# A gated cross-attention block: the keys' bias scaled behind the first statistics, transposes of the identity ahead of the tokens' ones, and block 1's tokens loaded sooner

## The chip, the cores and the metric

The kernel runs on one core of a Trainium2 chip. A core has five engines with queues of their own: TensorE (PE in the profile, with its weight loads as PEld), VectorE (DVE), ScalarE (ACT), GpSimd (POOL) and SyncE (SP), which here only issues DMA transfers. ScalarE issues a few transfers too. An engine takes its instructions in order; between engines there are semaphores. The metric is device microseconds of one execution, lower is better.

## The reference, cut to what matters

Tokens x are two sequences of 2048 rows with 512 features; the context has 77 rows per sequence. There are 16 heads of 32.

```python
x = x + tanh(g_xattn) * attention(layernorm(x), ctx, ctx)   # Wq, Wk, Wv, Wo with biases
x = x + tanh(g_ffn)   * ffn(layernorm(x))

# attention
q = layernorm(x) @ Wq.T + bq;  k = ctx @ Wk.T + bk;  v = ctx @ Wv.T + bv
out = softmax(q k.T / sqrt(32)) v @ Wo.T + bo

# ffn: both linear layers on integers, one scale for a whole tensor
def qlinear(x, w, b):
    sx, sw = max|x| / 127, max|w| / 127
    return (round(x / sx) @ round(w / sw).T + b) * (sw * sx)
out = qlinear(gelu(qlinear(x, w1, b1)), w2, b2)
```

Since the scale of a tensor is its greatest magnitude over all tokens, the whole attention has to be done before the first product of the feed-forward part, and that before the second product.

## The kernel before, in words

The 4096 tokens are eight blocks of 512 (`TB`), a block being four tiles of 128 rows. The first four blocks are the first sequence. Attention is computed in float32. For each block there are eight steps, two for each group of four heads: scores (`scores`, row ps in the profile), the least of them (mx), the exponential (e) on ScalarE, the sums and their reciprocals (sm, rs) on VectorE, the shares on GpSimd (row L561), their transposes through TensorE (pta), the product with the values (pc), and the product with Wo (oa, ob). Two steps are in flight. The feed-forward part follows: first product (ph), GELU, and then the second (pf).

In the attention part the order of every engine, SP's queue with it, is the order in which the code is written (a manual schedule). An instruction whose operand is late holds all that stands behind it on its engine. That holds for GpSimd above all here: its queue is strictly in order of the text.

The start, as the code has it:

- Loads. SP and ScalarE issue block 0's tokens in four pieces (`load_x(0, pieces=NT, ...)`), ScalarE then the context of sequence 0, `bk_sb` and `bq_sb` (2 KB each). SP goes on with column groups of Wk and Wq (`load_group`), Wv, `bv_sb`, the last two groups of Wq, the context of sequence 1, block 1's tokens (`load_x(1)`), Wo, and small vectors. A transfer takes one of eight semaphores in turn, and the issue of one waits until the transfer eight places ahead has landed.
- Constants. GpSimd writes the identity (`make_identity`), which the transposes need, and clears the buffers of the keys.
- `nbk`, the keys' bias times minus the scale of the scores, is computed on GpSimd from `bk_sb` (line 755). Its only reader is `place_k` for the second sequence on ScalarE (line 253).
- A loop over the four tiles of block 0 (from line 757): `norm_stats(0, t)` takes mean and variance on VectorE (st_a, mv) and the inverse sigma on GpSimd (lines 174 and 175: ve_a, then rstd); `normalize(0, t - 1)` makes xn on VectorE; `transpose_x(0, t - 1)` transposes it in four pieces through TensorE (ptx, line 344) and ScalarE copies it out (line 345); at the third and fourth pass `project_k` makes a group of the keys (pk, line 236).
- Then the keys are placed (`place_k`, kb, line 255 on VectorE), the other groups made, and `project_q(0, 0)` makes the first queries (pq, line 353).

The banks of PSUM matter at two places. `pt` has two, used in turn by the token transposes and later by the shares' transposes. `project_k` and `project_q` take turns on two others (`bank`), so a new product waits until the one two places ahead has been read.

Weights for the feed-forward part are rounded beside the attention; their loads come behind those named.

Of the kernel before, what the change touches and what calls it, by code (L numbers as in the profile page):

```python
# [8 lines left out]
F32 = mybir.dt.float32  # L9
BF16 = mybir.dt.bfloat16  # L10
AF = mybir.ActivationFunctionType
ALU = mybir.AluOpType
# [3 lines left out]
P = 128  # L16
D = 512
KC = D // P
# [20 lines left out]
SCALE = float(DK) ** -0.5  # L39
# [3 lines left out]
def tile_flamingo_gated_block(  # L43
# [21 lines left out]
    nc = tc.nc  # L65
# [6 lines left out]
    small = ctx.enter_context(tc.tile_pool(name="small", bufs=4))  # L72

    def big(name):
        return xpool.tile([P, KC, TB], F32, tag="xblk", name=name)
# [3 lines left out]
    def load_x(i, pieces=1, engines=(nc.sync,)):  # L79
        X[i] = big(f"x{i}")  # L80
        src = x[i * TB : (i + 1) * TB, :].rearrange("(t p) d -> p t d", p=P)
        n = NT // pieces
        for t in range(0, NT, n):
            engine = engines[t // n % len(engines)]
            engine.dma_start(X[i][:, t : t + n, :], src[:, t : t + n, :])

    def kchunks(w):
        return w.rearrange("(kc p) n -> p kc n", p=P)
# [17 lines left out]
    bk_sb = const.tile([P, KC], F32, name="bk_sb")  # L106
# [6 lines left out]
    def load_group(engine, dst, src, g):  # L113
        c = slice(g * P, (g + 1) * P)
        engine.dma_start(dst[:, :, c], kchunks(src)[:, :, c])

    def load_ctx(engine, b):
        engine.dma_start(ctx_sb[b], kchunks(ctxT[b]))
# [10 lines left out]
    load_group(nc.sync, wq_sb, wqT, 1)  # L129
    nc.sync.dma_start(wv_sb, kchunks(wvT))  # L130
    nc.sync.dma_start(bv_sb, bv.to_broadcast([NK, D]))
    for g in range(2, NG):
        load_group(nc.sync, wq_sb, wqT, g)
    for b in range(1, B):
        load_ctx(nc.sync, b)
    load_x(1)
    xT_sb = {}

    def load_xT(i):
# [11 lines left out]
    ident = const.tile([P, P], F32, name="ident")  # L151
# [66 lines left out]
    with actx:  # L218
        ps_s = actx.enter_context(tc.tile_pool(name="ps_s", bufs=2, space=PSUM))
        ps_t = actx.enter_context(tc.tile_pool(name="ps_t", bufs=2, space=PSUM))  # L220
# [3 lines left out]
        def bank(name):  # L224

            turn[0] += 1
            return ps_p.tile([P, D], F32, tag=f"pp{turn[0] % 2}", name=name)
# [4 lines left out]
        def project_k(b, g):  # L232

            pk = bank(f"pk{b}_{g}")
            for kc in range(KC):
                nc.tensor.matmul(
                    pk[:, :NK],
                    wk_sb[:, kc, g * P : (g + 1) * P],
                    ctx_sb[b][:, kc, :],
                    start=(kc == 0),  # L240
                    stop=(kc == KC - 1),
                )
            return pk

        def place_k(b, g, pk):

            for j in range(HG):
                r = slice(j * DK, (j + 1) * DK)
                dst = kblk[b][r, g, j % RT * NK : (j % RT + 1) * NK]
                bias = bk_sb[r, g : g + 1]  # L250
                if j % 2 and b > 0:
                    bias = nbk[r, g : g + 1]
                    nc.scalar.activation(dst, pk[r, :NK], AF.Identity, bias=bias, scale=-SCALE)
                else:
                    nc.vector.tensor_scalar(dst, pk[r, :NK], bias, -SCALE, ALU.add, ALU.mult)
# [18 lines left out]
        def norm_stats(i, t):  # L274

            if t == 0:
                ln[i] = (
                    small.tile([P, NT, 2], F32, tag="mv", name=f"mv{i}"),
                    small.tile([P, NT], F32, tag="rstd", name=f"rstd{i}"),
                )  # L280
            mv, rstd = ln[i]
            tile_stats(mv[:, t, :], X[i][:, t, :], f"a{i}_{t}")
            if i == 0:
                inverse_sigma(rstd[:, t : t + 1], mv[:, t : t + 1, :], f"a{i}_{t}")
            elif t == NT - 1:
                inverse_sigma(rstd, mv, f"a{i}")
# [45 lines left out]
        def normalize(i, t):  # L332
            mv, rstd = ln[i]
            xn[i, t] = work.tile([P, D], F32, tag="xn", name=f"xn{i}_{t}")
            nc.vector.tensor_scalar(
                xn[i, t], X[i][:, t, :], mv[:, t, 0:1], rstd[:, t : t + 1], ALU.subtract, ALU.mult
            )

        def transpose_x(i, t):
            if t == 0:  # L340
                xnT[i] = work.tile([P, KC, TB], F32, tag="xnT", name=f"xnT{i}", bufs=2)
            pt = ps_t.tile([P, KC, P], F32, tag="pt", name=f"ptx{i}_{t}")
            for kc in range(KC):
                nc.tensor.transpose(pt[:, kc, :], xn[i, t][:, kc * P : (kc + 1) * P], ident)
            nc.scalar.copy(xnT[i][:, :, t * P : (t + 1) * P], pt)
# [405 lines left out]
                    else:  # L751
                        task[0](*task[1:])

        nbk = small.tile([P, KC], F32, tag="nbk", name="nbk", bufs=1)
        nc.gpsimd.tensor_scalar(nbk, bk_sb, -SCALE, None, ALU.mult)
        pk = {}
        for t in range(NT + 1):
            if t < NT:
                norm_stats(0, t)
            if t > 0:  # L760
                normalize(0, t - 1)
                transpose_x(0, t - 1)
            if t in (2, 3):
                pk[t - 2] = project_k(0, t - 2)
        place_k(0, 0, pk[0])
        pk[2] = project_k(0, 2)
        place_k(0, 1, pk[1])
# [193 lines left out]
    with ExitStack() as fctx:  # L961
# [23 lines left out]
        for i in range(NB):  # L985
# [4 lines left out]
            for a in range(GT):  # L990
                G = gtile(f"G{i}_{a}")
                for v in range(GF // 2):
# [25 lines left out]
                    n = 1 if k == NB * GT * 2 - 1 else 2  # L1018
# [24 lines left out]
    for i in ends:  # L1043
# [37 lines left out]
        for t in range(NT):  # L1081
# [3 lines left out]
            n = 2 if i == ends[-1] and t == NT - 1 else 1  # L1085
# [73 lines left out]
```

## Time and profile before

| | |
|---|---|
| times of three runs | 634.09, 634.13, 636.54 us (median 634.13) |
| the profiled execution | 637.02 us, its span 634.8 us |
| TensorE busy | 599.1 us, 94% of the span |
| VectorE, ScalarE, GpSimd busy | 75%, 65%, 52% |
| granted TensorE clock, mean | 0.986 |
| first matmul of TensorE starts | 9.85 us |
| first queries (pq) on TensorE | 18.58 to 22.64 us |
| attention ends, feed-forward begins | about 401 us |

How to read it: the span runs from the first to the last instruction; the execution's own time is 2.2 us longer. The chain that ended last names, piece by piece, the work or the wait that set the time. A row of the timeline gives the start and the length in microseconds, the engine, the line of the kernel, the operation, what is written and read with the shape, the number of instructions, and in brackets how long the engine had been idle and who released it. The granted clock is the share of TensorE's full clock that the hardware let through. Releasers are inferred, and a few matmul records can be missing.

### The profile page before, as it was taken

To read this page: it belongs to the slowest core of one execution; us is meant where nothing else is said; L and a number is where in the kernel's file an instruction comes from. 1 tells how busy PE (TensorE), PEld (TensorE's weight loads), DVE (VectorE), ACT (ScalarE), POOL (GpSimd) and SP (SyncE) were. 2 spreads that over 40 slices of the span, in tenths; PEclk is the share of its full clock that TensorE was granted. 3 is DMA by queue.
4 is the path that set the end of the run, shared out by engine and by line. 5 is a ranking of instruction groups with operands and counts; after the bars stand their busy time and mean duration, and the time that the engine had idled before them with its cause. 6 is when DMAs were issued, how large, how long until landed. Compare 5 with 4: busy or idle time off the path is not lost.

```text
span 634.8 us, 9361 instructions
## 1 busy us (share of the span) xinstructions
PE 599.1 (94%) x3269; PEld 372.1 (59%) x3290; DVE 477.6 (75%) x743; ACT 410.9 (65%) x922; POOL 330.6 (52%) x291
## 2 busy tenths in 40 slices
PE   3999999899999999999999969799999979999997
PEld 3556467677777777787787745344444424444444
DVE  4376658678998788777757686999999789877452
ACT  1377556777667868766676641698989979554520
POOL 3066687679787789697785361000000009998000
PEclk9999999999999999999999969899999989999999
DMA  9910340031360163240000030299999019799942
GB/s 290 359 62 1 134 148 2 1 150 67 133 216 1 19 208 118 80 144 1 17 1 1 3 149 1 83 323 324 326 352 273 9 35 366 285 366 324 377 151 84
DMA packets 51270, 94.95 MB, mean 150 GB/s; under 512 B 22219, under 2 KB 26571, under 8 KB 45464
## 3 DMA queue, kind: packets, MB, share of 16 engines
q1 hardware_dynamic: 50120, 93.67, 42.9%
q10 hardware_dynamic: 1104, 0.69, 0.4%
q8 instruction: 26, 0.43, 0.3%
q14 instruction: 20, 0.16, 0.1%
HBM read 57.11 MB, written 33.57 MB: 143 GB/s over the span
## 4 chain that ended last, share of the span: by engine, by line
PE 77%; DVE 11%; POOL 4%; ACT 4%; issue 2%; DMA 1%; ACTq 0%; POOLq 0%; DVEq 0%
PE ph L1002 17%; PE pf L1069 17%; PE pta L572 7%; PE oa L443 6%; PE ps L523 5%; PE qa L443 5%; PE ob L443 5%; PE pc L581 4%; PE qb L443 4%; PE pq L353 3%; ACT e L543 2%; POOL e L561 1%; DVE sm L557 1%; PE po L598 1%; PE pvv L261 1%
## 5 line engine op out<-in xcount | busy, mean ns | idle before, releaser
L561 POOL TENSOR_TENSOR e<-e,rs 128x616 f32<-128x616 f32 x64 | 77.9, 1217 | 97.0 <-DVE rs L559 86.5
L543 ACT ACTIVATE e<-ps,mx 128x77 f32<-128x77 f32 x512 | 117.0, 344 | 12.8 <-DVE mx L532 9.6
L1069 PE MATMUL pf<-w2q,hq 128*128 128x512 bf16 (+1 forms) x518 | 111.8, 376 | 3.1 <-DVE hq L212 2.3
L1002 PE MATMUL ph<-xqT,w1q 128*128 128x512 bf16 x501 | 111.6, 382 | 2.6 <-DVE xqT L212 1.8
L1010 ACT ACTIVATE G<-ph,b1s,s 128x512 f32<-128x512 f32 x128 | 99.3, 778 | 13.6 <-PE ph L1002 2.9
L573 ACT COPY aT<-pta 77x512 f32<-77x512 f32 x128 | 68.8, 587 | 55.2 <-PE pta L572 55.1
L1069 PEld LDWEIGHTS <-hq 128*128 128x128 bf16 x528 | 51.8, 98 | 63.0 <-DVE hq L212 3.0
L1002 PEld LDWEIGHTS <-w1q 128*128 128x128 bf16 x512 | 50.5, 99 | 63.5 <-issue 4.2
L1020 DVE TENSOR_REDUCE hmax<-G 128x1 f32<-128x1024 f32 (+1 forms) x65 | 76.7, 1196 | 6.6 <-ACT G L1010 6.6
L572 PE MATMUL pta<-ident,e 128*77 128x128 f32 x512 | 72.4, 284 | 7.0 <-POOL e L561 4.0
L557 DVE TENSOR_REDUCE sm<-e 128x8 f32<-128x616 f32 x64 | 50.4, 788 | 24.1 <-ACT e L543 24.0
L572 PEld LDWEIGHTS pta<-ident,e 128*77 128x77 f32 x512 | 56.6, 149 | 19.2 <-issue 8.0
L532 DVE TENSOR_REDUCE mx<-ps 128x8 f32<-128x616 f32 x64 | 50.2, 786 | 22.4 <-PE ps L523 22.2
L1060 POOL TENSOR_SCALAR b_sb<-b_sb,s 128x512 f32<-128x512 f32 x1 | 3.5, 3486 | 122.0 <-issue 122.0
L1062 ACT ACTIVATE Gb<-Gb,inv_h 128x2048 f32<-128x2048 f32 x22 | 43.6, 1999 | 34.2 <-DMA Gb<-h 27.9
L523 PEld LDWEIGHTS ps<-kb,qT 64*128 64x128 f32 x512 | 36.0, 186 | 37.7 <-issue 31.0
L1083 POOL TENSOR_TENSOR x<-x,b_sb 128x512 f32<-128x512 f32 x32 | 57.2, 1826 | 0.1
L523 PE MATMUL ps<-kb,qT 64*128 64x154 f32 x512 | 50.6, 317 | 0.7 <-DVE qT L489 0.5
L1091 DVE SCALAR_TENSOR_TENSOR x<-pf,s,x 128x512 f32<-128x512 f32 (+1 forms) x33 | 23.8, 730 | 30.3 <-PE pf L1069 24.3
L624 DVE TENSOR_REDUCE xm<-x 128x1 f32<-128x512 f32 x64 | 40.8, 669 | 0.0
L1063 DVE TENSOR_SCALAR hq<-Gb 128x2048 bf16<-128x2048 f32 x22 | 36.6, 1697 | 5.6 <-ACT Gb L1062 5.6
L348 POOL TENSOR_TENSOR x<-x,bo_sb 128x512 f32<-128x512 f32 x32 | 40.4, 1272 | 0.0
(140 smaller groups left out, 940.5 us busy)
## 6 DMA issues: line engine op xcount, KB each, us to landing
h<-G SPq DMA_DIRECT2D x22, 1024.0 KB, 4.9
Gb<-h SPq DMA_DIRECT2D x22, 1024.0 KB, 8.6
out_y<-x SPq DMA_DIRECT2D x31, 256.0 KB, 4.0
x<-in_x SPq DMA_DIRECT2D x7, 1024.0 KB, 6.7
xT<-in_xT SPq DMA_DIRECT2D x6, 1024.0 KB, 8.9
raw_w<-in_w2T SPq DMA_DIRECT2D x6, 1024.0 KB, 6.5
raw_w<-in_w1T SPq DMA_DIRECT2D x4, 1024.0 KB, 12.8
w_dram<-xqT SPq DMA_DIRECT2D x4, 512.0 KB, 3.2
```

Of the source, the lines that this page charges most:

```text
L443: nc.tensor.matmul(ps[:, m * H : (m + 1) * H], a[:, c, m * P : (m + 1) * P], b[:, c, :], start=(m + c == 0 and not more), stop=(m + c == 2 ...
L523: nc.tensor.matmul(ps[:, q, u * RK : (u + 1) * RK], qT[i, g // 2][r, g % 2, t * P : (t + 1) * P], kblk[i // NBB][r, g, :], start=True, sto ...
L543: last = nc.scalar.activation(es[i, s][:, u, j * NK : (j + 1) * NK], sc[:, q, u, r, :], AF.Exp, bias=mx[:, q, u, r : r + 1], scale=-1.0,)
L557: nc.vector.tensor_reduce(sm, e4, AX.X, ALU.add)
L561: return nc.gpsimd.tensor_tensor(e4, e4, rs[:, :, :, None].to_broadcast([P, 2, HG, NK]), ALU.mult).ins
L572: nc.tensor.transpose(pt[:NK, j, :], es[i, s][:, u, j, :], ident)
L573: nc.scalar.copy(aT[i, g][:, :, t * P : (t + 1) * P], pt[:NK, :, :])
L1002: nc.tensor.matmul(ph[u], w1q[:, kc, fc * P : (fc + 1) * P], cur[:, kc, :], start=(kc == 0), stop=(kc == KC - 1),)
L1010: nc.scalar.activation(G[:, 2 * v + u, :], ph[u], AF.Gelu, bias=b1s[:, fc : fc + 1], scale=s1,)
L1020: nc.vector.tensor_reduce(hmax[:, k + u : k + u + 1], G[:, 2 * v + u : 2 * v + u + n, :], AX.XY, ALU.max, apply_absolute_value=True,)
L1069: nc.tensor.matmul(po[t, c.start][:, : c.stop - c.start], hq[:, fc, t * P : (t + 1) * P], w2q[:, fc, c], start=(fc == 0), stop=(fc == FC - 1),
L1083: nc.gpsimd.tensor_tensor(y, y, b2_sb, ALU.add)
```

## The change

Three edits, all in the start of the program.

- The two lines that make `nbk` move from ahead of the loop over block 0's tiles to behind it, so that on GpSimd the instruction stands behind the four pairs of ve_a and rstd.
- In their place 16 transposes of the identity by the identity go to TensorE. They write the four quarters of one `pt` bank in turn; nobody reads it. They wait for the identity alone.
- `load_x(1)` moves on SP's queue from behind context 1 to behind `bv_sb`, ahead of the last two groups of Wq and context 1.

```diff
     nc.sync.dma_start(wv_sb, kchunks(wvT))
     nc.sync.dma_start(bv_sb, bv.to_broadcast([NK, D]))
+    load_x(1)
     for g in range(2, NG):
         load_group(nc.sync, wq_sb, wqT, g)
     for b in range(1, B):
         load_ctx(nc.sync, b)
-    load_x(1)
     xT_sb = {}
...
-        nbk = small.tile([P, KC], F32, tag="nbk", name="nbk", bufs=1)
-        nc.gpsimd.tensor_scalar(nbk, bk_sb, -SCALE, None, ALU.mult)
+
+        run_up = ps_t.tile([P, KC, P], F32, tag="pt", name="run_up")
+        for n in range(16):
+            nc.tensor.transpose(run_up[:, n % KC, :], ident, ident)
         pk = {}
         for t in range(NT + 1):
             if t < NT:
                 norm_stats(0, t)
             if t > 0:
                 normalize(0, t - 1)
                 transpose_x(0, t - 1)
             if t in (2, 3):
                 pk[t - 2] = project_k(0, t - 2)
+        nbk = small.tile([P, KC], F32, tag="nbk", name="nbk", bufs=1)
+        nc.gpsimd.tensor_scalar(nbk, bk_sb, -SCALE, None, ALU.mult)
         place_k(0, 0, pk[0])
```

Apart from these, every engine issues the same instructions in the same order. The bank on which each later `pt` tile falls is the other one of the two.

## The prediction

> **What bounds the kernel now.** I read the page first, then the chain that ended last in order of time for the first 25 us, then the timeline of that stretch by engine, then the table of windows for TensorE's granted clock. The page's engine shares and its chain say that TensorE carries the kernel:
>
> ```profile
> PE 599.1 (94%) x3269; PEld 372.1 (59%) x3290; DVE 477.6 (75%) x743; ACT 410.9 (65%) x922; POOL 330.6 (52%) x291
> PE 77%; DVE 11%; POOL 4%; ACT 4%; issue 2%; DMA 1%; ACTq 0%; POOLq 0%; DVEq 0%
> ```
>
> PE is busy 94% of the span, so whatever starts it sooner should move the rest with it. The change touches only the start, and there the chain (start, length, what) goes through a 2 KB load:
>
> ```profile
> 2.11 5.81 DMA bk_sb<-in_bk
> 8.01 0.23 POOL nbk L755
> 8.32 0.25 POOL ve_a L174
> 8.64 0.58 POOL rstd L175
> 9.25 0.55 DVE xn L335
> 11.10 1.12 PE ptx L344 x4
> 12.22 1.62 PE pk L236 x8
> 18.79 3.85 PE pq L353 x8
> 22.64 0.85 PE pk L236 x8
> ```
>
> The reader is to see two things. The keys' bias lands at 7.92, GpSimd scales it (nbk), and only then computes the first inverse sigma (ve_a, rstd) for tokens whose statistics were done long before. And the same product pk, 8 instructions, takes 1.62 us at 12.22 and 0.85 us at 22.64. In the timeline of VectorE and GpSimd (start, length) the wait stands as its own number:
>
> ```profile
> 4.91 0.18 DVE L168 BATCH_NORM_AGGREGATE mv<-st_a 128x2 f32<-128x6 f32 x1
> 5.71 0.18 DVE L168 BATCH_NORM_AGGREGATE mv<-st_a 128x2 f32<-128x6 f32 x1
> 8.01 0.23 POOL L755 TENSOR_SCALAR nbk<-bk_sb 128x4 f32<-128x4 f32 x1 [5.60 <-DMA bk_sb<-in_bk]
> 9.25 0.55 DVE L335 TENSOR_SCALAR xn<-x,mv,rstd 128x512 f32<-128x512 f32 x1 [3.36 <-POOL rstd L175]
> ```
>
> The first statistics are there at 5.09 (4.91 + 0.18), the second at 5.89. GpSimd sits 5.60 us behind the load.
>
> The clock: the granted clock stands at 1.00 in the first 20 us, yet the first pq instruction lasts 1053 ns and its fellows 592, and instructions start 0.86 us apart before 19.4 and 0.43 after it. So TensorE ran at half speed from its first instruction at 9.85 to about 19.4. Later the table of windows does show such changes (from, to and length; PE's busy time and instructions; granted clock; DMA share and GB/s):
>
> ```profile
> 370.80:371.00 0.20, 0.00 (x0) 0.97 0.76 328
> 381.20:381.40 0.20, 0.20 (x2) 0.93 0.00 0
> 401.60:401.80 0.20, 0.05 (x1) 0.77 0.00 0
> 405.00:405.20 0.20, 0.20 (x2) 0.70 0.00 0
> 374.41:377.82 3.41, 2.35 (x9) 0.50 0.00 0
> 394.88:398.30 3.42, 1.75 (x12) 1.00 0.00 0
> 367.58:370.99 3.41, 1.73 (x12) 1.00 0.86 332
> ```
>
> From the partial shares the clock halves at 370.99, doubles at 381.23, halves at 401.71, doubles at 405.12. The distances are 10.24, 20.48 and 3.41 us: 3, 6 and 1 times 3.413. So the clock is judged on a grid of 3.413 us, and 103 steps back from 370.99 is 19.4, where the start became fast. The last three rows are whole steps of that grid.
>
> **The change part by part.**
>
> *The bias scaled later.* Removed from GpSimd's path: the wait on the load. The first ve_a can start when the statistics are there: 5.09 plus the 0.08 that lies between nbk's end (8.24) and ve_a (8.32) is 5.17 in place of 8.32: 3.15 us sooner. The xn chain behind it follows by its own rows: xn at 6.1, transposes (ptx) at 6.7 in place of 9.85. What is late next? Tokens 2 and 3 were issued at about 1.2 and landed 3.9 to 4.4 us later, at 5.6 at the latest; VectorE wants the third piece at 6.56 (9.71 - 3.15). Product pk of group 0 needs context (issued 1.63, landed 6.1 later: 7.73) and wk group 0 (1.67 + 6.5 = 8.17); it would come at 9.07 (12.22 - 3.15). wk 2 lands at 10.4, wq 0 at 9.6, wq 1 at 11.9, wv at 14.85, each before its shifted use. So the whole 3.15 us goes through, even with the half clock. The moved nbk, 0.23 us, now runs after the fourth rstd at about 9.9 (13.08 - 3.15); GpSimd's next work is the shares at 28.66 less the shift, and nbk's first reader is ScalarE's key placement at 52.68. It costs nothing, by 12 us of idle GpSimd; without that cover it would be 0.3.
>
> *Sixteen transposes of the identity.* The identity is written by 1.84 (1.55 + 0.29), and TensorE has nothing before 6.7. A ptx transpose of the same form starts every 0.2125 us (0.85 for 4 in the chain): 16 are 3.4 us, from 1.95 to 5.35: free. The other end is the full length of one, 421 ns, if they did not overlap: 6.7 us, to 8.7, which would hold the tokens' transposes 2.0 us and leave 1.15 of the gain. I take 0.2125, as the tokens' own transposes into one bank go at that pace. run_up shifts the two transposing banks by one; the third token transpose waits for ScalarE's copy of the first, as before.
>
> What they may bring is the clock. If it is full from the first token transposes, ptx falls from 0.85 to 0.45 (0.45 at 49.45 for 4), pk from 1.62 to 0.85. But then VectorE is late next: xn 3 ends at 10.5 (13.66 - 3.15), and pk's bank of group 0 is read only behind it (1.23 us, row L255), to 11.8. So pk 2 starts at 11.8, the second placement ends at 13.0, and pq 0, which takes that bank, runs 13.05 to 16.5 at 0.43 each. Before it ended at 22.64: 6.1 us, of which 2.95 are the clock's. In the profiled grid the steps end at 2.35, 5.76, 9.18: the 16 transposes fill 3.0 of the 3.41 us before 5.76 (0.88).
>
> Does such a step open the clock? No row shows it; the rows bound it. For: opening after 377.82:381.23 (filled) and after 517.74:521.18 (pf from 518.47: 0.79), and the 12 plain transposes alone of 394.88:398.30 kept the clock at 1.00, where 1.73 us of half-empty work at 367.58 lost it. Against: 374.41:377.82, 2.35 us, mostly transposes, did not open it, nor did 12.6 to 16.0, all busy with ptx and pk. I take it that a step filled to 0.88 opens it, by the rows at 0.79 and 1.00. Then the step to 9.18 holds only 0.4 of work; should it close, pk 0's end, ptx 2, pk 1 and ptx 3 go at half speed until 12.6, of which about 0.5 us reaches pq 0, the rest being VectorE's wait anyway.
>
> [...]
>
> *Block 1's tokens sooner.* On SP the 1 MB load goes from behind to before wq 2, wq 3 and context 1: about 9.23 in place of 11.24. Everything ahead of it, wv and bv, is untouched. All four had landed by 20.5 (11.24 + 9.3) and have the same bytes in sum; wq 2 is first read at 35.81 (29.7 after the shift), context 1 at 50.16, and the tokens' statistics at 34.04. Behind it, wo keeps its place; w1's first piece, landed 30.9 and read at 59.16, may slip by a microsecond. Both ways nothing, with 9 us of cover.
>
> *Behind 24 us* no wait on a load ends last until the weights of w1, which lie 28 us early, so the shift travels to the end.
>
> **Sum.** Profiled execution: 637.02 (span 634.8 and 2.2 around it) - 3.15 - 2.95 = 630.9. The three timed runs have a median of 634.13, 2.9 lower. Where the grid falls differs from run to run, and part of that 2.9 can be half-clock time at the start, which can't be saved twice. I take 5.3 of the 6.1 off the median: **628.8 us**.
>
> **The rivals.**
>
> 1. *The identity's transposes do not open the clock.* Speaks for: 374.41:377.82 and 12.6 to 16.0. Speaks against: 394.88:398.30. Then the start only shifts by 3.15: 634.13 - 3.15 = 631.0. Chance 0.33. [...]
>
> 2. *The transposes do not overlap* and hold the tokens' own: 1.15 is left: 633.0. Against it the pace of every ptx row. Chance 0.05.
>
> 3. *The gain is given back in block 0*, where the chain leaves TensorE from 33 to 57 us for GpSimd's wq_total and the shares. For: PE fills only 2.40 of the step 53.53:56.94. Against: all of it waits on computed things, which shift too. 634.1. Chance 0.07.
>
> 4. *Slower: the clock closes where it now stays open.* Place: those stalls from 33 to 57. Price: a step at half clock of dense work loses 1.7 us (half of 3.41). With the sixteen of no use it takes two such steps to eat the 3.15, and four to be slower by 0.5%: 634.13 - 3.15 + 6.8 = 637.8. Against: all those steps now show 1.00 with 2.40 to 2.81 us of work, and a shift by 3 to 6 us does not thin them. Chance 0.05.
>
> My forecast has 0.5, its own range 626.8 (all 6.1, and half a step luckier elsewhere) to 630.8.
>
> **How the numbers follow.** 0.5% is 3.2 us, about what a measurement of this kernel can tell from no change; 631.0 is thus the border. Faster: nearly all of the forecast's 0.5 and half of rival 1: 0.65. Slower: 0.05. The rest, 0.30, is within. The range takes in the forecast and rival 1 with a microsecond for the grid: 626.8 to 632.2; rivals 2 to 4 lie beyond its upper end.
>
> **What would show it.** First rstd near 5.5 and nbk behind the fourth; first token transposes near 6.7 (later: rival 2); pk at 0.85 or 1.62 for 8 and pq's first instruction at 592 or 1053 ns (the clock); pq 0 ending near 16.5, or 19 to 20 under rival 1; the end earlier by the same amount (if less, rival 3 or 4). I am wrong if an early load comes later than in this trace, since wk 0 at 8.17 leaves 0.2 us where the clock is full.

## The result and the profile after

The changed kernel takes 632.22 us (median of 14 runs, 630.92 to 634.81) against 635.03 for the kernel before (median of 14, 634.09 to 636.86). The ratio is 0.9951, 95% interval 0.9937 to 0.9964: 2.8 to 3.1 us or half a percent faster, where 5.3 us were forecast. The time is 0.02 us above the upper end of the range. Rival 1, a shift by 3.15 alone, comes nearest by its gain; its time of 631.0 is 1.2 us lower, since it was taken off 634.13, the median of three runs, and fourteen have 635.03. The profiled execution takes 632.68 us, its span 630.8.

The page of the changed kernel, busy time by engine and shares of the chain that ended last:

```profile
PE 603.1 (96%) x3306; PEld 374.6 (59%) x3306; DVE 478.4 (76%) x743; ACT 410.7 (65%) x922; POOL 329.8 (52%) x291
PE 78%; DVE 10%; ACT 5%; POOL 5%; issue 1%; DMA 1%; POOLq 0%; DVEq 0%; ACTq 0%
```

The chain in order of time at its start (start, length, what):

```profile
0.72 3.40 DMA x<-in_x
...
5.15 0.26 POOL ve_a L174
5.48 0.58 POOL rstd L175
6.09 0.55 DVE xn L335
...
8.03 1.09 PE ptx L344 x4
9.12 1.62 PE pk L236 x8
10.74 0.85 PE ptx L344 x4
11.59 1.62 PE pk L236 x8
13.21 0.85 PE ptx L344 x4
14.06 1.04 PE pk L236 x8
15.10 3.48 PE pq L353 x8
18.58 0.85 PE pk L236 x8
19.43 1.25 PE ps L523 x16
```

The wait for the bias is gone: the chain starts with the tokens, the first rstd stands at 5.48 in place of 8.64, the second token transposes at 8.03 in place of 11.10. But pk still takes 1.62 us for 8 instructions at 9.12, where the one at 18.58 takes 0.85, and only the third pk, at 14.06 with 1.04, is faster in part. The sixteen transposes did not open the clock here. Later changes of the granted clock, read from the table of windows as before (369.31, 376.14, 396.62, 400.03), lie 6.83, 20.48 and 3.41 us apart, which is 2, 6 and 1 times 3.413: a grid again, at another position. In each of the thirteen profiles of this case the changes that the table shows lie whole steps of 3.413 us apart, within 0.02 us. Counted back from 369.31, an estimate for a stretch in which the table itself shows no change, steps end here at 4.09, 7.50, 10.91 and 14.33. The same table by these steps (from and to, length, PE's busy time and instructions, the clock, which shows 1.00 until its first recorded change, and DMA):

```profile
0.67:4.09 3.42, 2.20 (x11) 1.00 0.68 213
4.09:7.50 3.41, 2.29 (x11) 1.00 1.14 315
7.50:10.91 3.41, 3.18 (x16) 1.00 1.18 328
10.91:14.33 3.42, 3.42 (x19) 1.00 1.05 335
```

The sixteen start at 1.89, 0.21 us apart, and end near 5.3. They fall into two steps, 2.20 us in the one and 1.2 in the other (where the first token transposes make up the rest of the 2.29 in the row), and fill neither. The step that opened the clock is the one to 14.33: the instructions of the third pk fall from 417 ns each to 275, and those of the fourth have 230 to 275.

### The profile page after: what moved, and what is told of

The parts are those of the page before. It is cut to its first block, busy times and chain, and to the rows that moved or that the text cites. A ratio compares the mean times of both kernels' runs of the same rounds, so it can differ in the third digit from the quotient of the medians.

```text
span 630.8 us, 9414 instructions
## 1 busy us (share of the span) xinstructions
PE 603.1 (96%) x3306; PEld 374.6 (59%) x3306; DVE 478.4 (76%) x743; ACT 410.7 (65%) x922; POOL 329.8 (52%) x291
## 4 chain that ended last, share of the span: by engine, by line
PE 78%; DVE 10%; ACT 5%; POOL 5%; issue 1%; DMA 1%; POOLq 0%; DVEq 0%; ACTq 0%
PE pf L1073 18%; PE ph L1006 17%; PE pta L572 7%; PE oa L443 6%; PE qa L443 5%; PE ps L523 5%; PE ob L443 5%; PE pc L581 4%; PE qb L443 4%; PE pq L353 3%; ACT e L543 3%; POOL e L561 2%; DVE sm L557 1%; PE po L598 1%; PE pvv L261 1%
## 5 line engine op out<-in xcount | busy, mean ns | idle before, releaser
L1073 PE MATMUL pf<-w2q,hq 128*128 128x512 bf16 (+1 forms) x528 | 113.7, 379 | 2.0 <-DVE hq L212 1.8
```

The source lines that it names most:

```text
L1073: nc.tensor.matmul(po[t, c.start][:, : c.stop - c.start], hq[:, fc, t * P : (t + 1) * P], w2q[:, fc, c], start=(fc == 0), stop=(fc == FC - 1),
```

## The experiments

Three theories. A: the clock is opened by a step of the grid that is about three quarters full (an estimate, from the step filled to 0.79 that opened it in the kernel before), transposes count, and sixteen of them (3.4 us in all) do that only where the grid happens to lie well; a step that is too empty closes the clock again, as the one from 367.58 with 1.73 us of work did there. B: transposes don't count as work, so no number of them opens the clock. C: the load of block 1's tokens at its new place takes back a part of the gain.

### The bias alone

The two lines of `nbk` behind the loop; no `run_up`, `load_x(1)` at its old place.

```diff
-        nbk = small.tile([P, KC], F32, tag="nbk", name="nbk", bufs=1)
-        nc.gpsimd.tensor_scalar(nbk, bk_sb, -SCALE, None, ALU.mult)
         pk = {}
...
+        nbk = small.tile([P, KC], F32, tag="nbk", name="nbk", bufs=1)
+        nc.gpsimd.tensor_scalar(nbk, bk_sb, -SCALE, None, ALU.mult)
         place_k(0, 0, pk[0])
```

> The bias is scaled behind the statistics; there are no transposes of the identity, and block 1's tokens stay where they were. Theory A (the whole gain is the bias; the sixteen transposes fill a step of TensorE's clock grid too seldom, and the step behind them is too empty to keep the clock): 3.15 us under the kernel before, that is 631.9 for a median of 635.0, and within 0.7 of the changed kernel's 632.2. Theory B (transposes never count as work for the clock): the same 631.9. Theory C (the earlier load of block 1's tokens takes back a part): 0.5 us or more under the changed kernel. In the profile of all three: first rstd near 5.5, first token transposes near 6.7.

Measured: 632.83 us (8 runs, 630.81 to 635.29), ratio 0.9967 (0.9947 to 0.9986) to the kernel before, run beside it with a median of 635.31. The first rstd comes at 5.36, the first token transposes at 6.58.

### The change without the sixteen transposes

```diff
-        run_up = ps_t.tile([P, KC, P], F32, tag="pt", name="run_up")
-        for n in range(16):
-            nc.tensor.transpose(run_up[:, n % KC, :], ident, ident)
```

> The changed kernel without the sixteen transposes of the identity. Theory A: equal to the changed kernel or up to 0.7 us slower, 632.2 to 632.9. Theory B: equal within the error. Theory C: slower than the bias alone by 0.5 us or more, since only the order of the loads tells the two apart. If the sixteen transposes were worth what was forecast for them, this kernel would be 2 us or more slower than the changed one.

Measured: 632.02 us (8 runs, 631.25 to 635.21), ratio 0.9957 (0.9943 to 0.9971). The three kernels with the bias moved have 632.83, 632.02 and 632.22, and their intervals overlap: moving the bias alone is worth 2.5 us, most or all of the gain, and what the sixteen and the earlier load add is under what these runs can tell. That the earlier load costs something (C) has no support here: the kernel without it is not faster. The two kernels spread over 4 us from run to run.

### 44 transposes in the kernel before

```diff
         nc.gpsimd.tensor_scalar(nbk, bk_sb, -SCALE, None, ALU.mult)
+        run_up = ps_t.tile([P, KC, P], F32, tag="pt", name="run_up")
+        for n in range(44):
+            nc.tensor.transpose(run_up[:, n % KC, :], ident, ident)
```

> The kernel before with 44 transposes of the identity in the 8 us that TensorE waits; bias and loads as before. They cover at least one whole step of 3.413 us and last until the tokens' transposes. Theory A: the clock is open when those start: 0.45 us for 4, 0.85 for 8 of pk, the first pq 592 ns, and pq 0 ends 2 to 3 us sooner, so 632 to 633 against 635.0. Theory B: pk stays at 1.62 and the 44 take 9.35 us, to 11.2, which holds the tokens by 1.4: 635.0 to 636.5.

Measured: 633.94 us (10 runs, 633.03 to 636.08), ratio 0.9983 (0.9971 to 0.9994). The timeline of TensorE in this kernel:

```profile
1.89 6.63 PE L758 MATMUL run_up<-ident 128*128 128x128 f32 x44 [1.89 <-POOL ident masks.py:199]
9.62 0.66 PE L344 MATMUL ptx<-ident,xn 128*128 128x128 f32 x4 [1.10 <-DVE xn L335]
...
11.43 1.25 PE L236 MATMUL pk<-ctx,wk_sb 128*128 128x77 f32 x8
12.47 1.06 PE L344 MATMUL ptx<-ident,xn 128*128 128x128 f32 x4
13.32 1.83 PE L236 MATMUL pk<-ctx,wk_sb 128*128 128x77 f32 x8
...
15.64 1.01 PE L236 MATMUL pk<-ctx,wk_sb 128*128 128x77 f32 x8
```

and its steps in the table of windows:

```profile
1.83:5.24 3.41, 3.35 (x16) 1.00 0.99 327
5.24:8.65 3.41, 3.28 (x30) 1.00 1.15 305
8.65:12.06 3.41, 1.76 (x15) 1.00 1.14 352
12.06:15.47 3.41, 3.41 (x19) 0.50 1.10 354
```

This decides against B. Sixteen records begin or run in the full step to 5.24 and 30 in the next, at twice the pace; all 44 take 6.63 us, not the 9.35 that they would at 0.2125 each. Nothing but transposes had run. The first tokens' transposes then last 0.66 us for 4 with their tail, where a group of 4 has 1.06 in the kernel before and 1.11 in the changed one. And the other half of A shows as well: the step to 12.06 holds 1.76 us, and the clock, now recorded, falls to 0.50 at its end. The second pk is back at half speed (1.83 with its tail) and only the third is fast. So the gain is 1.4 of the 2 to 3 us expected.

### 24 transposes, and fillers behind them

`fill(n)` issues n transposes of the identity into a bank of the scores' pool that is free at the start.

```diff
-        run_up = ps_t.tile([P, KC, P], F32, tag="pt", name="run_up")
-        for n in range(16):
-            nc.tensor.transpose(run_up[:, n % KC, :], ident, ident)
+        filler = ps_s.tile([P, NR, 512], F32, tag="ps", name="filler")
...
+        fill(24)
...
                 transpose_x(0, t - 1)
+            if t == 1:
+                fill(6)
...
+        fill(6)
         pk[2] = project_k(0, 2)
+        fill(3)
         place_k(0, 1, pk[1])
```

> The changed kernel with 24 transposes of the identity in place of sixteen, and with 6 more behind the first token transposes, 6 ahead of pk 2 and 3 ahead of pq 0, so that no step up to pq 0 is left half empty. Theory A: clock open from about 5.3 to 8.7 on, pk 0.85 for 8, pq 0 ends near 16.5 to 17.5 in place of 18.6: 629 to 631. Theory B: the added transposes run at half clock, the second token transposes come 1 us late, and the time is 633 or more.

Measured: 630.77 us (5 runs, 630.20 to 630.81), ratio 0.9929 (0.9917 to 0.9941). Its chain shows the pace of the full clock from the first token transposes (0.44 us for 4, 0.85 for a pk), and pq 0 ends at 16.59, where the prediction had put it with the clock open (16.5):

```profile
6.94 0.44 PE ptx L344 x4
...
8.54 0.85 PE pk L236 x8
...
13.08 3.51 PE pq L353 x8
16.59 0.85 PE pk L236 x8
17.44 1.25 PE ps L523 x16
```

The five runs spread over 0.6 us, where the kernel before, run beside them, spreads over 3.0: with the clock open from the first token transposes, most of what differed between runs is gone.

### 24 transposes, no fillers

```diff
-            if t == 1:
-                fill(6)
...
-        fill(6)
         pk[2] = project_k(0, 2)
-        fill(3)
```

> The changed kernel with 24 transposes of the identity in place of sixteen, and none behind them. Theory A (a step must be filled to open the clock, and the next ones must not be too empty): 24 last to 6.7 and fill one step to three quarters in any position, so the clock opens between 4 and 9; but the steps behind hold the two token transposes of 0.45 us and little else until pk, so it closes again in a part of the runs: between the two, 631 to 632.2, with pq 0 ending between 16.5 and 18.6. Rival (only the length of the run-up was lacking): as the filled kernel, 630.8, in all runs.

Measured: 630.79 us (6 runs, 629.99 to 631.30), ratio 0.9917 (0.9895 to 0.9938) to a kernel before of 635.88, run beside this kernel and the three that follow. Here the rival was right and my theory's second half was not needed: the fillers add nothing that these runs show, the length of the run-up was lacking. At 0.2125 us each 24 last 5.1 us, 1.5 steps, so by this sum, an estimate, one step is at least three quarters full in any position. In the profiles of the four kernels with 24 it was quite full each time (the steps to 6.45, 6.76, 5.35 and 5.70), so the worst position was not seen. In this profile the tokens' transposes begin at 6.92, as the 24 end, so the step behind is not as empty as behind sixteen.

### The filled kernel with the load at its old place

```diff
-    load_x(1)
     for g in range(2, NG):
         load_group(nc.sync, wq_sb, wqT, g)
     for b in range(1, B):
         load_ctx(nc.sync, b)
+    load_x(1)
```

> The filled kernel with block 1's tokens at their old place on SP's queue. If the order of the loads is worth nothing: 630.8 within 0.4, as the filled kernel. Theory C (the earlier load takes back a part, or brings one): 0.5 us or more away from it.

Measured: 630.70 us (6 runs, 630.57 to 631.10), against 630.77 and 630.79 with the earlier load. The order of the loads is worth nothing that these runs can tell, about 0.4 us. C falls.

### Sixteen, and the fillers behind them

```diff
-        fill(24)
+        fill(16)
```

> The filled kernel with sixteen transposes of the identity ahead, as in the change, in place of 24; the 6, 6 and 3 behind stay. Theory A: sixteen end at 5.3 and leave 1.4 us empty ahead of the token transposes, so the clock opens one step later in about half the runs, and the added transposes then go at half clock: 630.8 to 632.5, more spread than the filled kernel. Rival (the length plays no part, it is the filling behind that counts): 630.8.

Measured: 631.81 us (6 runs, 630.67 to 632.32), ratio 0.9931 (0.9909 to 0.9953). That is 1 us above the kernels with 24 run beside it. The profiled execution is the fastest of the six, and in it the grid lay well (a step ended at 5.49, which the sixteen filled almost whole), and the token transposes took 0.66. That the four runs at 631.8 to 632.3 had a bad position fits theory A and was not seen, since they have no profile.

### Three more profiled executions of the changed kernel

No edit; what differs is where the grid lies.

> The changed kernel once more, for one look with the clock's grid at another position. Sixteen transposes run from 1.89 to 5.3. Theory A, by where a step of 3.413 us ends: between 4.4 and 6.2 (half of the positions) the sixteen fill it to three quarters or more and the first token transposes take 0.45 us for 4; the step behind it then holds 0.9 to 1.6 us of work, and the clock closes again at its end unless that is near half, so pk 0 or ptx 2 go at half clock; pq 0 ends between 17 and 18.6. Outside: nothing is opened, pk 0 takes 1.62, pq 0 ends between 17.5 and 21. Theory B: ptx 0 takes 0.85 in any position.

> The same as the look before, at one more position of the grid: 0.45 us for the first four token transposes and a closing behind them if a step ends between 4.4 and 6.2, else 0.85 and no closing (theory A); 0.85 in any position (theory B).

> The same as the two looks before, at one more position of the grid.

Measured: 631.29, 631.31 and 633.90 us, beside a kernel before of 633.86 on the same chip. In the first two a step ended at 6.16 and 6.19. The table of windows of the first:

```profile
2.75:6.16 3.41, 2.82 (x14) 1.00 1.08 361
6.16:9.58 3.42, 2.05 (x17) 1.00 1.18 303
```

and of the third, where a step ended at 6.46:

```profile
3.05:6.46 3.41, 2.52 (x12) 1.00 1.00 329
6.46:9.87 3.41, 2.71 (x12) 1.00 1.17 319
```

The grid lies 0.3 us apart in the two. In the first the sixteen fill their step to 2.55 us (2.75 to 5.3; the table counts the tail of the last; 2.52 in the second), the clock opens at its end, the first pk takes 0.85 us and the scores (ps) start at 17.66. In the third they fill 2.25, nothing opens, every pk takes 1.62 and the scores start at 20.70. The closing that theory A expected behind an opened step did not come in the first two: 2.05 us in the step to 9.58 kept the clock open, and the second pk, behind that step, takes 0.85 us as well.

### The filled kernel, and the junction to the feed-forward part

Ahead of the first feed-forward product TensorE waits for VectorE, and the clock had closed there in every profile so far (at 401.71 in the kernel before, 396.62 in the changed one, 395.57 in the filled one). 16 transposes on either side of the small product that spreads the tokens' maximum:

```diff
+        fillers.append(ps_s.tile([P, NR, 512], F32, tag="ps", name="filler2"))
+        fill(16)
         s_x, inv_x = scale_of(diagonal_of(xm.rearrange("p n b t -> p (n b t)"), "x"), "x", ps_p, "pp0")
+        fill(16)
```

> The filled kernel, and 16 more transposes of the identity on either side of the product that spreads the tokens' greatest magnitude, where TensorE waits for VectorE ahead of the first feed-forward product and starts it at half clock for one step of 3.41 us. Theory A: the clock stays open there; a step of dense work at half clock costs 1.7 us: 629.1, and the first ph instructions start 0.22 us apart in place of 0.43. Theory B (transposes don't count): the clock closes as before and the time is 630.8 or more.

Measured: 628.57 us (6 runs, 627.44 to 629.60), ratio 0.9883 (0.9860 to 0.9905): 2.2 us under the filled kernel. The table of windows at the junction, first of the filled kernel, then of this one:

```profile
390.00:395.00 5.00, 1.68 (x11) 1.00 0.00 0
395.00:400.00 5.00, 4.38 (x13) 0.66 0.00 0
```

```profile
390.00:395.00 5.00, 4.64 (x40) 1.00 0.00 0
395.00:400.00 5.00, 4.53 (x22) 1.00 0.02 3
```

With the wait filled the clock does not close: the row from 395 shows 1.00, where the filled kernel has 0.66. In the 5 us from 395 there are 20 instructions of the first product in place of 13 (two of the 22 in the row are fillers). The first three take 0.81 us together, where the first three in the kernel before, at half clock, take 1.44; the product also starts 0.35 us earlier. This is the fastest of all kernels run, 1.2% under the kernel before.

### Where the time is made

From the profiles: the start of the scores (the first ps of the chain) and the span.

| kernel | ps starts | span | difference |
|---|---|---|---|
| before | 23.49 | 634.8 | 611.3 |
| changed | 19.43 | 630.8 | 611.4 |
| changed, first further execution | 17.66 | 629.5 | 611.8 |
| changed, third further execution | 20.70 | 632.1 | 611.4 |
| bias alone | 18.07 | 629.0 | 610.9 |
| change without the sixteen | 18.50 | 629.7 | 611.2 |
| filled | 17.44 | 628.7 | 611.3 |
| filled, and the junction | 17.46 | 627.0 | 609.5 |

Behind the first scores all take 611.4 us within half a microsecond, but for the last, which was edited there. What the start gains reaches the end whole.

## Why the prediction was right or wrong

*The bias: right.* The first rstd came at 5.48 (forecast near 5.5), the first token transposes at 6.69 (6.7), nbk at 9.99 behind the fourth rstd. No load came late. The shift of 3.15 is in the profile, and the kernels with it but without the sixteen are 2.5 and 3.3 us under the kernel before by their medians.

*The earlier load: right,* worth nothing that the runs can tell, though its side effect was larger than said: w1's first piece is issued at 20.50 in place of 18.43, 2 us and not one. Nobody waits for it in the profile.

*The pace of the sixteen: right.* They go at 0.21 us each and end at 5.3, before the tokens' transposes; rival 2 is out.

*The clock: the wrong step.* "I take it that a step filled to 0.88 opens it" was right about the clock and wrong about the kernel. A step that full does open it (44 transposes alone, which filled 3.35 of 3.41 us, 24, and sixteen where they fill 2.52 or more of the 3.41), but 0.88 was the filling at the grid position of one execution, that of the kernel before. I wrote that the position differs from run to run and used it only to trim the sum, by 0.8, and not for this term, where it decides whether the 2.95 are there at all. The sixteen are 3.4 us long, one step; at nearly every position they straddle two, and in the changed kernel's profile they filled 2.20 and 1.2. Of the five positions that the profiles show (4.09, 6.16, 6.19, 6.46 and, with fillers, 5.49), two did not open. The prediction's own figures would have shown it: to fill a step to 0.79, the least that had a row, by transposes from 1.95 to 5.35, its end has to lie between 4.6 and 6.1, which is 1.4 of 3.41 us. By 2.52 us (0.74), the least filling by the sixteen that opened it in these runs, it is about half of the positions. The other fear of that paragraph was misjudged as well: it put 0.4 us of work into the step behind, but the second token transposes and a part of pk fall there too, and where sixteen had opened the clock that step held 2.05 and kept it.

*The term's size, and the time it was taken off.* The 2.95 were the half-clock time of one execution, the one of 637.02 whose first scores start at 23.49. For that execution the sum was right: with the clock open from the first token transposes the filled kernel has a span of 628.7, and 634.8 - 3.15 - 2.95 is 628.7. A median gains less, since kernels without any run-up have good positions too: their scores start at 18.07 and 18.50 in the two profiles, against 17.66 in the first further execution of the changed kernel, where the sixteen opened the clock. The prediction allowed 0.8 for that, which leaves 2.15. Run beside the filled kernel, the two kernels without a run-up are 2.1 and 1.3 us above it, so 2.15 is at the upper end of what an open clock is worth to a median here. But the 634.13 from which 5.3 were taken was low: longer series of the kernel before have 635.0, 635.3 and 635.9. So 628.8 was out of reach even with the clock open: of 17 runs with 24 transposes and the junction as it was, the lowest is 629.99.

What the sixteen did bring: 16 runs without them average 632.8, 14 with them 632.2. The difference of 0.6 is below what these runs resolve; whether the sixteen are worth a few tenths stays open, but the 2.15 left in the forecast would have shown.

*Rival 1* has the gain nearest to the result, 3.15 against 2.8 us, but not for its reason. (By time alone rival 2's 633.0 is nearer, through the low 634.13.) It said that transposes do not open the clock. By the kernel with 44 of them they do: nothing else had run when the pace doubled at 5.24, from 16 records in a step to 30. The prediction's own evidence against opening, the step 12.6 to 16.0 of the kernel before, has another reading: it held 0.85 us of transposes and 2.56 of pk, while the step 10.91 to 14.33 of the changed kernel, which opened the clock, held 1.53 of transposes and 1.89 of pk. So a pk seems to count for less of its time than a transpose. Two more steps fit: in the change without the sixteen the one from 8.56 to 11.97 (1.28 and 2.12 by its chain) opened the clock, in the third further execution the one from 9.87 to 13.28 (0.85 and 2.56) did not. With the line for opening between 2.25 and 2.52 us of transposes, these steps put a pk's time at 0.46 to 0.65 of a transpose's, an estimate; it is read from four steps and was not tried by itself.

*Rivals 3 and 4* did not occur in any profile: the table above leaves no room for a loss in block 0. But two of the fourteen runs of the changed kernel, 632.90 and 634.81 us, have a mean granted clock of 0.980 and 0.978, where the others have 0.984 to 0.986. A step of 3.41 us at half clock is 0.0027 of the whole, so by this sum, an estimate, they had about two and three closed steps more than the rest. They have no profile, and where the clock closed is not known; a closing behind the sixteen, as in the kernel with 44, is one possibility.

## What to carry to other kernels

Look for the first use of a tiny load, placed early in a queue: here it held everything written behind it on GpSimd, and the first rstd came at 8.64 in place of 5.48. The chain showed it as 5.81 us of a 2 KB transfer, and moving the instruction behind the urgent ones cost nothing here, since its own reader came 38 us later. If TensorE's clock is to be opened by filler work, try a filler of one and a half steps of the clock's grid up to the moment at which real work begins: 24 float32 transposes, 5.1 us, had the clock open for the first token transposes in all four profiles with them, while sixteen, 3.4 us or one step's worth, had it open in three of five, by where the grid lay. The same fillers paid 2.2 us at the one other wait where they were tried, ahead of the dense feed-forward product.

## What the runs showed that I had not expected

Plain float32 transposes counted as work for the clock: 44 of them opened it at 5.24, the end of the first step that they filled (3.35 of 3.41 us). The line between opening and not was narrow in these runs: 2.52 us of transposes in a step of 3.41 opened it, 2.25 did not. For closing they show no line: 1.76 us of busy time in a step closed it in the kernel with 44, while 1.75 (394.88 in the kernel before) and 2.05 (the first further execution) kept it open, so busy time alone does not place it. And most of the 3 us by which runs of the kernel before differ seem to come from the first 20 us: with 24 transposes ahead the spread of runs fell to 0.5 to 1.3 us in three kernels, and to 2.2 in the one with the filled junction.
